# Softmax denominators of a transformer layer's masked attention: pair sums on VectorE and many ones-matmuls replaced by accumulating DMAs and one ones-matmul per run of eight steps

## Chip, cores, metric

One core of a Trainium2 chip. The metric is the device time of one execution of the whole kernel in microseconds (us), median of several runs.

## The reference, cut to what matters

Sixteen batches of 1024 nodes and 256 channels pass through three graph attention layers and one transformer layer with masked attention of eight heads. Only the latter's attention is changed.

```python
scores = jnp.einsum('fnhd,fmhd->fhnm', q, k) / jnp.sqrt(jnp.asarray(D, x.dtype))   # H = 8, D = 32
scores = jnp.where((adj > 0)[None, None, :, :], scores, -1e9)
attn = jax.nn.softmax(scores, axis=-1)
t = jnp.einsum('fhnm,fmhd->fnhd', attn, v).reshape(F, N, C)
```

The kernel computes exp(score) without a maximum, multiplies by the mask, and needs two sums over the 1024 keys: weights times values, and the weights alone (the denominator).

## The kernel before

A batch has four combinations of head group `g` (four heads) and half `hf` (512 queries), and each has eight steps `jt` of 128 keys. A step makes four 128x512 tiles of weights, two to a buffer `pa`. A *quad* is four matmuls (eight instructions in the trace), one for each head, side by side in the array's column groups.

```python
def paired(g, hf):
    return g == 1 or hf == 1          # three of the four combinations
...
for n in range(len(steps) + LAG):
    m = n - LAG                       # the value quad runs two steps behind the scores
    if m >= 0:
        both = not paired(g, hf)      # not paired: a ones quad at every step
        pe((1 + both) * 0.855, lambda: value(m, both), accs[g, hf], pas[m] + [va(jt)], ...)
        if not both and jt % 2:       # paired: a ones quad at every other step, from the pair sum
            pe(0.855, lambda: quad(accs[g, hf][1], jt, lambda r: ss[r // 2].t[:, r % 2, :], lambda r: ones, ...))
    ...                               # scores on TensorE, exp on ScalarE, mask on VectorE, into pas[n]
    if paired(g, hf) and jt % 2:
        sums[n] = [r_sums.new() for _ in range(2)]
        for ss, p0, p1 in zip(sums[n], pas[n - 1], pas[n]):
            dve(tt_us(2 * HALF), lambda: nc.vector.tensor_add(ss.t, p0.t, p1.t), [ss], [p0, p1])
```

(`...` marks cuts.) Nothing is emitted at once: `pe`, `dve`, `act`, `dma` record work with a planned duration, and a list scheduler at build time chooses each engine's fixed order from these and from constants (`BIAS` is its weight for changes of the array's mode; `GATS`, `VALUES`, `STEPS`, `FEED` spread each stage over the batches). Batches overlap: while one is in its attention, others are in graph attention or in the feed-forward part. The attentions of two batches hardly overlap, because keys, values and the transposed input have one buffer each.

## Time and profile before

| | before |
|---|---|
| time, median | 4240.8 us (4238.5 to 4245.0) |
| busy: TensorE, VectorE, ScalarE, GpSimd | 98%, 88%, 54%, 8% of the span |
| ones quads | 320, of 0.86 us each |
| pair additions on VectorE | 384, 457 us |
| DMA engines, mean of 16 | 22% |

The lines behind this table are in the prediction. It is read as one full engine, TensorE, with VectorE close behind and the DMA engines largely free: it invites moving additions to the DMA engines.

### The profile page before, as it was taken

The page shows a single profiled execution, that of the slowest core. Times are in us where ns is not written, and L with a number is a line of the kernel's source. Part 1 is how long each engine was busy: PE and PEld are TensorE (multiplying, and loading weights), DVE is VectorE, ACT ScalarE, POOL GpSimd, SP SyncE. Part 2 cuts the span into 40 slices and gives each one's busy share as a digit, 9 for nine tenths or more (in the row PEclk, how much of TensorE's full clock was granted, in tenths as well). Part 3 has the DMA queues.
Part 4 walks back from the last instruction along what each step waited for, and adds up shares of the span by engine and source line. Part 5 has one row for each costly group of instructions (what it writes and reads, how often), then busy time and mean ns, then how long its engine had stood idle before and what let it go on. Part 6 is the DMA issues. An engine that isn't in the chain of part 4 may idle for free.

```text
span 4234.8 us, 68471 instructions
## 1 busy us (share of the span) xinstructions
PE 4144.4 (98%) x24738; PEld 2385.9 (56%) x24738; DVE 3713.0 (88%) x6786; ACT 2307.1 (54%) x5041; POOL 351.7 (8%) x391
## 2 busy tenths in 40 slices
PE   7999999999999999999999999999999999999997
PEld 3746466564655646556464665646556465564642
DVE  7589898997989889898998989989898898988977
ACT  2445555554655645556555555656556455565564
POOL 0000010010100100001000100101001000010000
PEclk9999999999999999999999999999999999999998
DMA  3121222212222122221212222122212222212131
GB/s 103 50 66 36 76 66 66 56 46 70 68 75 53 50 66 61 81 63 56 60 48 75 66 66 56 50 66 71 76 52 60 56 60 81 64 52 60 47 82 39
DMA packets 180682, 263.82 MB, mean 62 GB/s; under 512 B 41328, under 2 KB 76400, under 8 KB 180336
## 3 DMA queue, kind: packets, MB, share of 16 engines
q1 hardware_dynamic: 180336, 259.36, 22.2%
q8 instruction: 198, 3.24, 0.3%
q14 instruction: 148, 1.21, 0.1%
HBM read 91.03 MB, written 33.95 MB: 30 GB/s over the span
## 4 chain that ended last, share of the span: by engine, by line
PE 73%; DVE 12%; ACT 7%; issue 3%; DMA 3%; POOL 2%; SPq 1%; DVEq 0%; ACTq 0%; POOLq 0%
PE bank L787 19%; PE bank L1094 12%; PE bank L861 9%; PE sc L1221 9%; PE bank L1327 5%; PE bank L871 5%; PE bank L663 4%; PE bank L460 4%; PE sc L1010 4%; DVE pa L1254 3%; DVE pt L760 2%; POOL rstd L412 2%; ACT hn L431 2%; ACT hna L431 2%; PE sc L1046 2%
## 5 line engine op out<-in xcount | busy, mean ns | idle before, releaser
L1245 ACT ACTIVATE pa<-sc 128x512 f32<-128x512 f32 x2048 | 1093.7, 608 | 610.3 <-PE sc L1221 524.7
L1254 DVE TENSOR_TENSOR pa<-pa,mask 128x1024 f32<-128x1024 f32 x1024 | 1220.2, 1215 | 48.5 <-ACT pa L1245 48.4
L760 DVE SCALAR_TENSOR_TENSOR pt<-row,e,mask 128x512 f32<-128x512 f32 x1536 | 1054.9, 744 | 90.7 <-DMA row<-rd 55.8
L787 PE MATMUL bank<-qb,pt 128*128 128x257 f32 x4096 | 940.9, 382 | 1.0 <-DVE pt L760 0.5
L787 PEld LDWEIGHTS bank<-qb,pt 128*128 128x128 f32 x4096 | 767.7, 190 | 197.5 <-ACT pa L1245 40.0
L1221 PE MATMUL sc<-qs,ks 128*128 128x512 f32 x2048 | 682.0, 446 | 2.9 <-ACT pa L1245 2.1
L1094 PE MATMUL bank<-pa,va 128*32 128x512 f32 x4096 | 533.0, 597 | 3.6 <-DVE pa L1254 3.2
L861 PE MATMUL bank<-pt,qb 128*32 128x512 f32 x4096 | 515.4, 595 | 7.3 <-DVE pt L760 6.7
L1221 PEld LDWEIGHTS sc<-qs,ks 128*128 128x128 f32 x2048 | 363.6, 188 | 237.1 <-ACT pa L1245 93.7
L1269 DVE TENSOR_TENSOR sums<-pa,pa 128x1024 f32<-128x1024 f32 x384 | 457.0, 1214 | 0.3 <-PE bank L1094 0.2
L663 PE MATMUL bank<-w_aug,hT 128*128 128x259 f32 (+1 forms) x1536 | 374.3, 388 | 4.3 <-ACT e L674 3.6
L815 ACT ACTIVATE ex<-bank,rec 128x256 f32<-128x256 f32 x256 | 122.1, 477 | 437.5 <-DVE rec L807 396.1
L663 PEld LDWEIGHTS bank<-w_aug,hT 128*128 128x128 f32 x1536 | 286.2, 191 | 74.0 <-issue 12.8
L412 POOL TENSOR_TENSOR rstd<-rstd,neg_half 128x4 f32<-128x4 f32 x160 | 203.1, 1272 | 1468.6 <-DVE rstd L409 1417.4
L861 PEld LDWEIGHTS bank<-pt,qb 128*32 128x32 f32 x4096 | 127.1, 109 | 310.0 <-issue 214.5
L871 PE MATMUL bank<-pt,e 128*32 128x512 f32 x2048 | 292.1, 592 | 0.0
L1094 PEld LDWEIGHTS bank<-pa,va 128*32 128x32 f32 x4096 | 116.2, 109 | 267.7 <-issue 208.7
L1010 PE MATMUL sc<-hTa,wqkv_sb 128*128 128x512 f32 x512 | 240.1, 596 | 4.6 <-ACT hTa L995 4.6
L431 ACT ACTIVATE hn<-xt,mv,rstd 128x256 f32<-128x256 f32 x384 | 206.3, 601 | 40.4 <-DVE mv L421 39.6
L892 ACT COPY ot<-bank 128x512 f32<-128x512 f32 x128 | 74.8, 586 | 257.7 <-PE bank L861 215.3
L1094 PE MATMUL bank<-sums,ones 128*32 128x512 f32 x1536 | 208.0, 596 | 0.8
L403 DVE BATCH_NORM_STATS2 stg<-xt 128x6 f32<-128x256 f32 x512 | 205.4, 414 | 3.2
(107 smaller groups left out, 3993.7 us busy)
## 6 DMA issues: line engine op xcount, KB each, us to landing
row<-rd SPq DMA_DIRECT2D x192, 256.0 KB
ks<-hi SPq DMA_DIRECT2D x512, 64.0 KB
ks<-lo SPq DMA_DIRECT2D x512, 64.0 KB
qs<-hi SPq DMA_DIRECT2D x512, 64.0 KB
qs<-lo SPq DMA_DIRECT2D x512, 64.0 KB
xt<-in_x_dram SPq DMA_DIRECT2D x32, 512.0 KB
x<-xt SPq DMA_DIRECT2D x32, 512.0 KB
xr<-x SPq DMA_DIRECT2D x64, 256.0 KB
```

The lines of the kernel that those rows point to most:

```text
L431: lambda: nc.scalar.activation(dst, src, func, bias=bias, scale=scale),
L663: nc.tensor.matmul(g.t[:, : C + 3 * H], hT.t[:, ct, k * P : (k + 1) * P], w_aug[l][:, ct, :], start=ct == 0, stop=ct == CT - 1,)
L760: lambda: nc.vector.scalar_tensor_tensor(pt.t, row.t, e3[:, 2, jt // TH, h, jt % TH : jt % TH + 1], mask[:, jt, hf * HALF : (hf + 1) * HAL ...
L787: nc.tensor.matmul(g.t[:, : D + 1], pts[jt].t[:, k * P : (k + 1) * P], qb[:, jt, 0, :], start=jt == 0, stop=jt == NT - 1,)
L861: nc.tensor.matmul(g.t[u * D + d : u * D + d + D3, :], qb[:, j, h + u, d : d + D3], pts[u][j - jt].t, start=j == 0, stop=j == NT - 1,)
L871: nc.tensor.matmul(gd.t[c : c + D3, :], one(jt + k, h + u).to_broadcast([P, D3]), pts[u][k].t, start=jt == 0, stop=jt == NT - 2,)
L1010: nc.tensor.matmul(sc.t, wqkv_sb[:, ct, c0 : c0 + P], hT.t[:, ct, hf * HALF : (hf + 1) * HALF], start=ct == 0, stop=ct == CT - 1,)
L1094: nc.tensor.matmul(ac.t[r * D3 : (r + 1) * D3, :], columns(r), of_head(r), start=first, stop=last,)
L1221: nc.tensor.matmul(scs[r - r0].t, ks.t[:, r, jt * P : (jt + 1) * P].bitcast(F32R), q.t[:, r, :].bitcast(F32R), start=True, stop=True,)
L1245: lambda: nc.scalar.activation(pt.t[:, v, :], sc.t, AF.Exp, scale=1.0 / math.sqrt(D3)),
L1254: lambda: nc.vector.tensor_mul(pt.t, pt.t, mask[:, jt : jt + 1, i0 : i0 + HALF].to_broadcast([P, 2, HALF]),),
L1269: lambda: nc.vector.tensor_add(ss.t, p0.t, p1.t),
```

## The change

Its intent: let the DMA engines add the eight steps' weights in SBUF, so that VectorE has no pair sums and TensorE multiplies by ones once per combination, 64 quads instead of 320.

```diff
-BIAS = 0.516
+BIAS = 0.211
-    GATS = (0.0, 0.388), (0.388, 0.271), (0.659, 0.201)
-    VALUES, STEPS, FEED = (1.132, 0.099), (1.231, 0.63), (2.355, 0.252)
+    GATS = (0.0, 0.375), (0.375, 0.244), (0.619, 0.227)
+    VALUES, STEPS, FEED = (0.94, 0.302), (1.242, 0.561), (2.172, 0.546)
...
+        RUN = 8
...
+                first = jt % RUN == 0
+                if first:
+                    sums[g, hf] = [r_sums.new() for _ in range(2)]
+                for ss, pt in zip(sums[g, hf], pas[m]):
+                    if first:
+                        dma(1.5, lambda: nc.sync.dma_start(ss.t, pt.t), [ss], [pt])
+                    else:
+                        dma(2.4, lambda: nc.gpsimd.dma_start(ss.t, pt.t, accum_op=ALU.add),
+                            [ss], [pt], us=1.1, engine="pool")
                 pe(
-                    (1 + both) * 0.855,
+                    0.855,                         # the value quad alone
...
-                if not both and jt % 2:
-                    ss = sums[m]
+                if jt % RUN == RUN - 1:
+                    ss = sums[g, hf]               # one ones quad per combination
...
-                if paired(g, hf) and jt % 2:       # the pair additions on VectorE
-                    ...
```

(Long calls are joined to one line and cuts are marked.)

More of the change, by code (lines that the diff above doesn't have):

```diff
@@ L1090, in attention, with quad @@
         pas, accs, sums = {}, {}, {}
-        def quad(ac, jt, of_head, columns, first, last):
+        def quad(ac, of_head, columns, first, last):
             for r in range(HG):
@@ L1100, in quad @@
                 )
-        def value(n, both):
-            g, hf, jt = steps[n]
-            for ac in accs[g, hf][: 1 + both]:
-                quad(
-                    ac,
-                    jt,
-                    lambda r: pas[n][r // 2].t[:, r % 2, :],
-                    lambda r: (
-                        ones
-                        if ac is accs[g, hf][1]
-                        else va.t[:, jt, (g * HG + r) * D3 : (g * HG + r + 1) * D3]
-                    ),
-                    jt == 0,
-                    jt == NT - 1,
-                )
-        def paired(g, hf):
-            return g == 1 or hf == 1
+        RUN = 8
         rec.stream(b + STEPS[0], STEPS[1])
@@ L1131, in attention @@
                     accs[g, hf] = [r_bank.new(), r_bank.new()]
-                both = not paired(g, hf)
-                pe(
-                    (1 + both) * 0.855,
-                    lambda: value(m, both),
-                    accs[g, hf],
+                first = jt % RUN == 0
[3 more added lines that the diff above has]
+                    if first:
+                        dma(
+                            1.5,
+                            lambda: nc.sync.dma_start(ss.t, pt.t),
+                            [ss],
+                            [pt],
+                        )
+                    else:
+                        dma(
+                            2.4,
+                            lambda: nc.gpsimd.dma_start(ss.t, pt.t, accum_op=ALU.add),
+                            [ss],
+                            [pt],
+                            us=1.1,
+                            engine="pool",
+                        )
+                pe(
+                    0.855,
+                    lambda: quad(
+                        accs[g, hf][0],
+                        lambda r: pas[m][r // 2].t[:, r % 2, :],
+                        lambda r: va.t[:, jt, (g * HG + r) * D3 : (g * HG + r + 1) * D3],
+                        jt == 0,
+                        jt == NT - 1,
+                    ),
+                    [accs[g, hf][0]],
                     pas[m] + [va(jt)],
@@ L1145, in attention @@
                             accs[g, hf][1],
-                            jt,
                             lambda r: ss[r // 2].t[:, r % 2, :],
                             lambda r: ones,
-                            jt == 1,
+                            jt == RUN - 1,
                             jt == NT - 1,
@@ L1263, in attention @@
                             )
-                if paired(g, hf) and jt % 2:
-                    sums[n] = [r_sums.new() for _ in range(2)]
-                    for ss, p0, p1 in zip(sums[n], pas[n - 1], pas[n]):
-                        dve(
-                            tt_us(2 * HALF),
-                            lambda: nc.vector.tensor_add(ss.t, p0.t, p1.t),
-                            [ss],
-                            [p0, p1],
-                        )
         watch(b_rec, b_rec.t, 1)
```

## The prediction

> **What bounds the kernel now.** I read the page first: shares of busy time, then the chain that ended last, then the costliest groups.
>
> ```profile
> PE 4144.4 (98%) x24738; PEld 2385.9 (56%) x24738; DVE 3713.0 (88%) x6786; ACT 2307.1 (54%) x5041; POOL 351.7 (8%) x391
> q1 hardware_dynamic: 180336, 259.36, 22.2%
> PE 73%; DVE 12%; ACT 7%; issue 3%; DMA 3%; POOL 2%; SPq 1%; DVEq 0%; ACTq 0%; POOLq 0%
> ```
>
> TensorE (PE) is busy for 98% of the span, and 73% of the chain is its own work. VectorE (DVE) follows at 88% and has its own part of the chain; GpSimd (POOL) and the DMA engines are mostly free. So time taken off TensorE should come off the end, as long as nothing else becomes the bound. Since busy time of matmuls overlaps, I take their real cost from the timeline, not from the groups. The groups (each shape apart) give the counts:
>
> ```profile
> L1269 DVE TENSOR_TENSOR sums<-pa,pa 128x1024 f32<-128x1024 f32 x384 | 457.0, 1214 | 0.3 <-PE bank L1094 0.2
> L1094 PE MATMUL bank<-sums,ones 128*32 128x512 f32 x1536 | 208.0, 596 | 0.8
> L1094 PE MATMUL bank<-pa,ones 128*32 128x512 f32 x1024 | 142.3, 592 | 0.0
> ```
>
> The matrices of ones form the softmax denominators: 1536 matmul instructions from pair sums that VectorE makes (three of the four head group and half combinations) and 1024 straight from the weights (the fourth). The timeline of TensorE in the middle of the run gives the pace:
>
> ```profile
> 2054.19 1.04 PE L1094 MATMUL bank<-pa,va 128*32 128x512 f32 x8
> 2055.05 1.04 PE L1094 MATMUL bank<-pa,ones 128*32 128x512 f32 x8
> 2055.91 1.04 PE L1094 MATMUL bank<-pa,va 128*32 128x512 f32 x8
> 2056.77 1.04 PE L1094 MATMUL bank<-pa,ones 128*32 128x512 f32 x8
> ```
>
> Columns are start, duration, engine, line, operation, tiles, shapes, count. The duration shown is 1.04 us, but the next group of eight (a quad: four heads, two instructions each) starts 0.86 us later. A quad costs **0.86 us** of TensorE.
>
> The last view is again TensorE's timeline, at a batch boundary, for the scores (the attention's first product):
>
> ```profile
> 2009.99 0.73 PE L1221 MATMUL sc<-qs,ks 128*128 128x512 f32 x2
> ...
> 2218.77 1.27 PE L1221 MATMUL sc<-qs,ks 128*128 128x512 f32 x4
> ...
> 2265.92 0.73 PE L1221 MATMUL sc<-qs,ks 128*128 128x512 f32 x2
> ```
>
> One batch's 32 attention steps take from 2010 to 2220, some 210 us; then 46 us pass before the next batch's first score. Other layers' work fills TensorE all the while. The mean is 4240/16 = 265 us a batch, or 210/32 = 6.6 us a step inside the attention. That matters for the rival below.
>
> **What the Trainium skill says.**
> 1. "DMA: Bandwidth & Descriptors", section "Rules for kernel authors": an accumulating DMA is issued from GpSimd, and reads its destination and writes it later, so that another accumulate into the same bytes must wait for the first one's semaphore. Each total is then a serial chain of eight transfers. The trace before has no accumulating DMA; no run shows it yet.
> 2. The same page, "Issuing engines are not separate DMA queues": transfers from GpSimd share the 16 engines with those from SyncE. The existing 22.2% must be added to the new load.
> 3. The same page, "Anatomy of one DMA — SWDGE (gpsimd) path": about 2.0 us fixed plus bytes over 436 GB/s. The trace agrees with the rate: in the start-up loads of the adjacency (512 KB each, as large as one accumulate) the DMA view of 20 to 36 us, in slices of 0.4 us, reads
>
> ```profile
> GB/s 243 300 294 225 230 225 246 415 384 451 440 389 440 379 461 266 102 20 0 0 0 0 0 0 0 21 72 297 389 410 190 128 113 138 154 251 369 364 394 358
> ```
>
> so 380 to 460 GB/s at best; I use 420.
> 4. "SBUF — State Buffer", "Who interferes with whom": a VectorE operation with two SBUF inputs contends with GpSimd's reads; descriptor generation needs the write side (the page calls it inferred). VectorE runs almost nothing but such operations here, so I expect little blocking of the new issues; no run shows it yet.
>
> **The change part by part.**
> *Removed from TensorE.* Before: (1536 + 1024)/8 = 320 quads of ones. After: one per head group and half, 4 x 16 batches = 64. Removed: 256 x 0.86 = **220 us**, all on the path that sets the end: 4240 - 220 = 4020.
> *Removed from VectorE.* 384 additions at 1.19 us busy each, 457 us: 3713 - 457 = 3256, 81% of 4020. In the stretches where the chain runs over VectorE this keeps TensorE fed, but TensorE's idle time is only 4235 - 4144 = 90 us, so it can be worth 90 us at most; I count 20.
> *Added to GpSimd.* Per batch 4 runs x 8 steps x 2 tiles = 64 transfers, 8 of them plain copies from SyncE and 56 accumulates: 896 accumulates in all. At the 1.1 us the program itself plans for an issue, 986 us; with 352 that is 1338 us, 33%. Not a bound.
> *Added to the DMA engines.* A copy moves 512 KB: 0.524 MB/420 GB/s = 1.25 us. An accumulate must read source and destination: I estimate twice that, 2.5 us (the program plans 2.4). Per batch 56 x 2.5 + 8 x 1.25 = 150 us. Existing: 22.2% of 265 = 59 us. Sum 209 us of a 251 us batch, 83%. Not over, but high, and an estimate.
> *Moved.* Planning constants are retuned, above all a smaller penalty (0.516 to 0.211) on mode changes of the array, which lets the schedule change modes more often. The program's table puts a change at about 0.1 us; I allow 20 us in all, an estimate without a view behind it.
>
> *The serial chain.* For each total: issue (1.1 us), 2.5 us of data, 1 to 2 us until the semaphore, thus about 5 us to the next. The two totals of a step overlap, but share engines: 2 x 2.5 = 5.0 us a step if nothing else moves, and 5.0/(1 - 0.22) = 6.4 us with SyncE's traffic at its mean share. A batch has 28 accumulating steps and 4 openings (wait for the closing quad, then a copy; I take 6 us): 28 x 6.4 + 24 = 203 us. With the 46 us between attentions this is 249 us, against TensorE's 4020/16 = 251. The two are **level** by my estimate, and that sets my range. The margin is 28 x 16 = 448 us of run time for each microsecond a step is longer, once the chain is the bound. Some overlap of the batch gap with the last run's tail helps; queueing hurts. Two engines level to 1% never mesh perfectly in a fixed instruction order: I add 80 us of waiting.
>
> Sum: 4240 - 220 - 20 + 20 + 80 = **4100 us**, 3.3% less.
>
> **The rivals.**
> *A: the accumulate is slower than planned and the chain becomes the bound.* For it: the order of instructions is fixed at build time from planned times; the weights' ring has six tiles, three steps, and a tile is now held until its transfer has landed, so that ScalarE and then TensorE stall behind a late one. The mean of all transfers in this trace is only 259 MB in 0.222 x 4235 us, 276 GB/s; at that rate an accumulate takes 3.8 us, a step 7.6 us plus SyncE's share, and a batch at least 28 x 7.6 + 24 + 46 = 283 us: 4530 us. Against it: those are mostly short packets; the new ones have 4 KB rows, and the 512 KB loads ran at 380 to 460.
> *B: the transfers delay others.* Row broadcasts from DRAM feed VectorE ("DMA row<-rd" already ends 55.8 us of VectorE's idle time, 31 times), and GpSimd, in order, now blocks on landings while rstd work queues behind it. For: 192 row loads and 160 rstd steps; 1 us each exposed would be 352 us. Against: TensorE always has work of another batch, and before the change it waited 12 us or less for anything. I would expect a quarter exposed: about 90 us, total 4110 to 4200 together with my waiting term.
> *C: nothing gets in the way.* TensorE stays at 98%: 4000 to 4030.
>
> **Range and chances.** C gives the lower end, 3990 with some of VectorE's relief. The centre, 4100, is level balance with some waiting. B alone lands near 4150 to 4200, about no change being 4155 to 4325. A starts at about 4350 and is open above. I weigh C 0.3, the centre 0.3, B 0.22, A 0.18. The constants in the diff (1.1, 2.4 and retuned spans) look like measured and fitted ones, which speaks against A; the close balance speaks for leaving it a fair share. That gives faster 0.70, same 0.14, slower 0.16, and 3990 to 4380 as a range for eight in ten.
>
> **What would show each step.** Right: 512 matmul instructions with ones instead of 2560, at 0.86 us a quad; no additions into sums on VectorE; VectorE busy about 3260; TensorE busy near 3920 and still 95% or more; DMA share near 80% of the attention's stretches; accumulates into one tile 5 to 6.5 us apart; scores of a batch within 210 us. Wrong by rival A: TensorE busy falls under 92%, ScalarE waits for DMA on pa, accumulates into one tile over 7 us apart, DMA near 90% throughout. Wrong by B: VectorE's wait for row grows from 56 us to several hundred, or its wait for rstd from 54 us. If accumulates cost clearly under 2.5 us of the engines, the result is C. The prediction fails if TensorE's work doesn't fall by the 220 us, or if GpSimd's issue costs 3 us instead of 1.1 (896 x 3 = 2700 us, and 6 us a step by itself).

## The result, and the profile after

4672.2 us (4667.0 to 4683.0, four runs) against 4240.8: ratio **1.1019**, 95% interval 1.0997 to 1.1042. The change is 10% slower; 3.3% faster had been predicted, and the time lies far outside the range. (A ratio here is the mean time of one kernel's runs over that of the other's of the same rounds, so not quite the ratio of the medians quoted.)

The page of the changed kernel: engines, DMA queues (packets, MB, share of 16 engines), the chain of waits by engine and by line, three groups, and the issues of the accumulates (count, KB each, us from issue to landing).

```profile
PE 4223.9 (90%) x22690; PEld 2371.7 (51%) x22690; DVE 3328.0 (71%) x6402; ACT 2331.7 (50%) x5041; POOL 1079.1 (23%) x1287
q0 software_dynamic: 129024, 469.82, 53.1%
q1 hardware_dynamic: 198768, 326.48, 23.4%
DMA 32%; PE 32%; DVE 20%; issue 7%; SPq 4%; ACT 3%; POOL 2%; DVEq 0%; ACTq 0%; POOLq 0%
L1250 ACT ACTIVATE pa<-sc 128x512 f32<-128x512 f32 x2048 | 1110.4, 602 | 861.3 <-DMA sums<-pa 489.5
L1127 POOL DMA_DIRECT2D sums<-pa x896 | 780.6, 877 | 2706.8 <-DVE pa L1259 894.1
L1094 PE MATMUL bank<-sums,ones 128*32 128x512 f32 x512 | 130.6, 693 | 76.1 <-DMA sums<-pa 55.3
sums<-pa POOLq DMA_DIRECT2D x896, 512.0 KB, 5.8
```

The work went where it was meant to: 512 ones instructions instead of 2560, VectorE 385 us less busy. But TensorE's share fell from 98% to 90%, and its own part of the chain from 73% to 32%; the DMA engines have 32% of the chain, by line mostly `sums<-pa`. ScalarE now stands idle 489.5 us for accumulates that have not released a `pa` buffer. The queue of the accumulates gives their price: 53.1% of 4673.4 us over 896 is **2.77 us of all 16 engines** each.

TensorE's busy time itself did not fall. It rose by 80 us, though 2048 matmul instructions are gone; in e1_drop (below), with the same instructions, it is 3945 us. The clock granted to TensorE was lower: 0.956 of full speed in the mean, against 0.995 before and 0.993 in e1_drop, and a ones matmul on `sums` took 693 ns in the mean, 596 before. If all of TensorE's work lay on the path, this would cost at most 3945 x (0.993/0.956 - 1) = 153 us, an estimate. The clock is lower in the slower runs of this series (0.978 in e14_three_quarters); no run parts it from the waits, so its share of the loss stays open.

The clearest view is the end of the run. Only the last batch's attention is left there, and nothing competes with it. GpSimd's timeline (start, duration of the issue, ..., idle before and what ended it), then the DMA view of 4565 to 4585 us:

```profile
4564.67 0.86 POOL L1127 DMA_DIRECT2D sums<-pa  x1 [1.59 <-DVE pa L1259]
4567.23 0.86 POOL L1127 DMA_DIRECT2D sums<-pa  x1 [1.69 <-DVE pa L1259]
4569.98 0.86 POOL L1127 DMA_DIRECT2D sums<-pa  x1 [1.89 <-DVE pa L1259]
4572.72 0.86 POOL L1127 DMA_DIRECT2D sums<-pa  x1 [1.88 <-DMA sums<-pa]
4575.48 0.86 POOL L1127 DMA_DIRECT2D sums<-pa  x1 [1.90 <-DMA sums<-pa]
```

```profile
DMA packets 1042, 3.83 MB, mean 191 GB/s; under 512 B 112, under 2 KB 112, under 8 KB 1040
q0 software_dynamic: 1040, 3.80, 99.0%
sums<-pa POOLq DMA_DIRECT2D x8, 512.0 KB, 5.0
```

One accumulate starts about every 2.75 us, the engines are 99% busy with them alone, and 512 KB per 2.75 us are the 191 GB/s. A step needs two, so no step of an attention can be shorter than 5.5 us, whatever TensorE does. The same stretch, from the last batch's first exp to the end, in the view by windows (length; busy us and instructions of each engine; TensorE's granted clock; DMA share; GB/s), before and after:

```profile
4060.00:4235.00 175.00, 149.12 (x688) 57.74 (x688) 141.86 (x217) 88.36 (x166) 13.04 (x11) 0.94 0.22 58
```

```profile
4418.00:4673.00 255.00, 171.30 (x558) 59.43 (x558) 116.12 (x178) 89.45 (x165) 58.33 (x66) 0.80 0.80 172
```

It takes 80 us longer with fewer instructions for TensorE and VectorE (TensorE's busy time grows, at a granted clock of 0.80 against 0.94); the DMA engines go from 22% to 80%. That is 80 of the 439 us between the two spans. The other 357 us are in the fifteen batches before: from the first exp of batch 0 to that of batch 15, ScalarE's timeline gives 3839 us before (255.9 a batch) and 4195 us after (279.7).

What the other transfers suffer shows in the list of waits (engine, line, what it waited for: us, times, longest), before:

```profile
DVE pt L760 <- DMA row<-rd: 55.8, 31, 8.1
DVE mv L421 <- POOL rstd L412: 54.2, 53, 1.1
DVE xr L1385 <- DMA xr<-x: 17.6, 17, 3.6
```

and after:

```profile
DVE xr L1381 <- DMA xr<-x: 226.5, 35, 10.5
DVE mv L421 <- POOL rstd L412: 126.0, 91, 3.8
DVE pt L760 <- DMA row<-rd: 116.6, 38, 8.0
PE sc L1226 <- DVE lo L1022: 108.3, 17, 9.2
```

### The profile page after: what moved, and what is told of

Its sections match the earlier page's. It is cut to its first block, busy times and chain, and to the rows that moved or that the text cites. A ratio compares the mean times of both kernels' runs of the same rounds, so it can differ in the third digit from the quotient of the medians.

```text
span 4673.4 us, 67023 instructions
## 1 busy us (share of the span) xinstructions
PE 4223.9 (90%) x22690; PEld 2371.7 (51%) x22690; DVE 3328.0 (71%) x6402; ACT 2331.7 (50%) x5041; POOL 1079.1 (23%) x1287
## 3 DMA queue, kind: packets, MB, share of 16 engines
q0 software_dynamic: 129024, 469.82, 53.1%
## 4 chain that ended last, share of the span: by engine, by line
DMA 32%; PE 32%; DVE 20%; issue 7%; SPq 4%; ACT 3%; POOL 2%; DVEq 0%; ACTq 0%; POOLq 0%
DMA sums<-pa 23%; DVE pt L760 9%; PE bank L787 6%; DVE pa L1259 5%; PE bank L1094 4%; SPq L1031 4%; PE bank L861 4%; DMA out_dram<-xr 4%; PE bank L663 3%; PE sc L1010 3%; PE sc L1226 3%; PE bank L460 3%; DMA row<-rd 2%; PE bank L1323 2%; DMA xr<-x 2%
## 5 line engine op out<-in xcount | busy, mean ns | idle before, releaser
L1250 ACT ACTIVATE pa<-sc 128x512 f32<-128x512 f32 x2048 | 1110.4, 602 | 861.3 <-DMA sums<-pa 489.5
L1127 POOL DMA_DIRECT2D sums<-pa x896 | 780.6, 877 | 2706.8 <-DVE pa L1259 894.1
L760 DVE SCALAR_TENSOR_TENSOR pt<-row,e,mask 128x512 f32<-128x512 f32 x1536 | 1055.5, 740 | 190.4 <-DMA row<-rd 116.6
L787 PE MATMUL bank<-qb,pt 128*128 128x257 f32 x4096 | 958.4, 384 | 3.8 <-DVE pt L760 3.8
L1226 PE MATMUL sc<-qs,ks 128*128 128x512 f32 x2048 | 737.0, 459 | 184.2 <-DVE lo L1022 108.3
L1094 PE MATMUL bank<-pa,va 128*32 128x512 f32 x4096 | 620.9, 616 | 43.1 <-DVE pa L1259 39.8
L663 PE MATMUL bank<-w_aug,hT 128*128 128x259 f32 (+1 forms) x1536 | 423.7, 424 | 62.6 <-ACT e L674 27.3
L663 PEld LDWEIGHTS bank<-w_aug,hT 128*128 128x128 f32 x1536 | 309.8, 210 | 190.0 <-ACT qb L685 57.0
L1010 PE MATMUL sc<-hTa,wqkv_sb 128*128 128x512 f32 x512 | 263.3, 639 | 3.7 <-ACT pa L1250 2.3
L1381 DVE TENSOR_TENSOR xr<-xr,row_c 128x512 f32<-128x512 f32 x64 | 43.5, 680 | 226.5 <-DMA xr<-x 226.5
L1094 PE MATMUL bank<-sums,ones 128*32 128x512 f32 x512 | 130.6, 693 | 76.1 <-DMA sums<-pa 55.3
```

The source lines that it names most:

```text
L663: nc.tensor.matmul(g.t[:, : C + 3 * H], hT.t[:, ct, k * P : (k + 1) * P], w_aug[l][:, ct, :], start=ct == 0, stop=ct == CT - 1,)
L760: lambda: nc.vector.scalar_tensor_tensor(pt.t, row.t, e3[:, 2, jt // TH, h, jt % TH : jt % TH + 1], mask[:, jt, hf * HALF : (hf + 1) * HAL ...
L787: nc.tensor.matmul(g.t[:, : D + 1], pts[jt].t[:, k * P : (k + 1) * P], qb[:, jt, 0, :], start=jt == 0, stop=jt == NT - 1,)
L1010: nc.tensor.matmul(sc.t, wqkv_sb[:, ct, c0 : c0 + P], hT.t[:, ct, hf * HALF : (hf + 1) * HALF], start=ct == 0, stop=ct == CT - 1,)
L1094: nc.tensor.matmul(ac.t[r * D3 : (r + 1) * D3, :], columns(r), of_head(r), start=first, stop=last,)
L1127: lambda: nc.gpsimd.dma_start(ss.t, pt.t, accum_op=ALU.add),
```

## The experiments

Theory **S**: the accumulates occupy the 16 DMA engines, and during an attention these become the bound. Rivals: **L**, the serial latency of issue, landing and semaphore in each chain; **C**, the retuned constants; **P**, a fixed order planned from too low costs. In runs that leave out or falsify the sums, the result is wrong, and two details are changed alike: the reciprocal of the denominator becomes an addition of 1 (no division by zero), and the switch to the general fallback is off. Each ratio is to the kernel before.

### The accumulates left out, or made plain copies

```diff
 e1_drop:   the else branch with nc.gpsimd.dma_start(..., accum_op=ALU.add) is removed
 e2_plain:
-    nc.gpsimd.dma_start(ss.t, pt.t, accum_op=ALU.add)
+    nc.gpsimd.dma_start(ss.t, pt.t)
```

> The 896 accumulates are left out, everything else of the change stays (order, constants, the 128 copies, one closing quad per run); the result is wrong on purpose. Theory S (the accumulates themselves, as transfers, cost the time): TensorE becomes the bound again, 4020 to 4090 us. Theory C (the retuned constants or the new order of TensorE are bad in themselves): above 4250 us.

Measured: 4068.9 us, 0.9596. The rest of the change keeps what was expected of it: 172 us less, of the 220 worked out. C is out as a cause of the loss.

> The same 896 transfers, from GpSimd and in the same serial chain, but as plain copies without addition; wrong result on purpose. Theory S, in the form that the read-modify-write occupies the 16 DMA engines twice as long as a copy (2.75 us against about 1.3): queue share falls from 53% to about 27%, time 4050 to 4250 us. Rival L (the serial latency of issue, landing and semaphore, not the occupation, sets the pace): landing falls only by 1 to 1.5 us, time stays above 4400 us.

Measured: 4155.6 us, 0.9800. The same 896 transfers in the same chains cost 87 us more than none; as accumulates they cost 603 us more. The page of this run:

```profile
q0 software_dynamic: 129024, 469.82, 29.4%
sums<-pa POOLq DMA_DIRECT2D x896, 512.0 KB, 3.5
```

29.4% of 4149.8 us over 896 is 1.36 us; an accumulate's 2.77 us is **2.03 times** a copy's. But landing fell too, from 5.8 to 3.5 us, and an issue from 0.86 to 0.53 us, so this run alone does not part S from L.

### The chains kept, the occupation varied

```diff
 e9_tiny, e13_half, e14_three_quarters with c = 8, 256, 384:
-    nc.gpsimd.dma_start(ss.t, pt.t, accum_op=ALU.add)
+    nc.gpsimd.dma_start(ss.t[:, :, :c], pt.t[:, :, :c], accum_op=ALU.add)
```

> The same 896 accumulates in the same serial chains and with the same waits, but each over 8 columns of 512 per half (about 1/64 of the bytes); wrong result on purpose. It keeps issue, landing and semaphore of every link and takes the engines' occupation away. Theory S (occupation of the 16 engines): within 2% of the run without accumulates, 4060 to 4150 us, although each link still takes some 3 us to land. Theory L (serial latency): above 4300 us.

Measured: 4083.9 us, 0.9632. Queue and landing (min, median, max) of this run:

```profile
q0 software_dynamic: 243712, 7.40, 9.8%
DMA to landing us min/median/max: 2.4/2.6/5.7
```

Every link still takes 2.6 us to land, with all its waits, plus 1.2 us of issue (0.86 in the change). With the occupation at 0.45 us, the chains cost 15 us in all over e1_drop. L is out in the sense that these fixed parts of a link are harmless by themselves.

> The change with accumulates over 256 of the 512 columns of each half; wrong result on purpose. Occupation should be about 1.4 us, as much as a whole plain copy's 1.36 us. If occupation alone decides, the time is that of the plain copies, 4130 to 4190 us; if reading and writing the destination costs more than the engines' time, above 4300 us.

> The same over 384 columns: occupation about 2.1 us. By the serial sum, a step is 2 x 2.1 us, over 0.77 with SyncE's share 5.5 us; 28 steps, 4 openings of 6 us and 67 us of gap are 245 us a batch, just under TensorE's 251: 4150 to 4350 us if there is a knee where the attention's transfers overtake TensorE's work; about 4400 us (halfway between 4156 and 4672) if the time grows in proportion to the occupation.

Measured: half the columns 4136.3 us (0.9751), three quarters 4363.2 us (1.0291). The occupations, from these queues, were higher than expected, 1.73 and 2.37 us; first half, then three quarters:

```profile
q0 software_dynamic: 243712, 234.94, 37.5%
```

```profile
q0 software_dynamic: 243712, 352.38, 48.8%
```

All runs with the order of the change, in order of occupation. The period is the mean distance between the first exps of successive batches (twelve in the middle), from ScalarE's timeline:

| run | occupation per transfer (queue share x span / 896) | landing, median | period of a batch | time |
|---|---|---|---|---|
| e1_drop | none | none | 246.9 us | 4068.9 us |
| e9_tiny | 0.45 us | 2.6 us | 245.1 | 4083.9 |
| e2_plain (copies) | 1.36 | 3.5 | 248.7 | 4155.6 |
| e13_half | 1.73 | 4.2 | 246.9 | 4136.3 |
| e14_three_quarters | 2.37 | 5.1 | 261.2 | 4363.2 |
| the change | 2.77 | 5.8 | 281.0 | 4672.2 |

There is a **knee** between 1.73 and 2.37 us. Below it the period stays at TensorE's 245 to 249 us; above it, 0.40 us more of occupation cost 309 us. If every one of the 896 waited its turn in full, it would be 358 us. Growth in proportion, the other expectation, would have put three quarters above 4400; the 4363 measured are nearer to the knee's range of 4150 to 4350, but 13 us outside it. The half run is 19 us faster than the copies though its transfers occupy the engines longer: occupation under the knee does not order these two, and what does stays open. Below the knee most of what the transfers cost lies in the last batch's attention, from its first exp to the end: 147 us in e1_drop, 185 in e9_tiny, 209 in e2_plain, 212 in e13_half. Landing grows along with occupation, so above the knee the two are not separate causes.

One batch in the middle of the run shows the two limits, in the view by windows: its attention (first exp to last), then the gap to the next batch's first exp. First e9_tiny, then the change:

```profile
1947.10:2135.40 188.30, 187.16 (x1095) 108.24 (x1097) 167.86 (x294) 111.39 (x244) 77.31 (x67) 1.00 0.38 79
2135.40:2192.10 56.70, 56.70 (x325) 35.63 (x318) 37.42 (x103) 31.90 (x73) 10.99 (x14) 1.00 0.42 103
```

```profile
2192.00:2414.60 222.60, 203.90 (x1123) 114.96 (x1123) 171.83 (x297) 112.62 (x243) 57.23 (x66) 0.96 0.84 184
2414.60:2477.40 62.80, 58.46 (x297) 33.83 (x292) 34.16 (x99) 32.49 (x73) 12.06 (x15) 0.92 0.59 134
```

In e9_tiny TensorE is busy throughout. In the change the attention is 34 us longer and the gap 6 us. Over twelve batches in the middle the DMA engines are busy for 85% of the attentions and 58% of the gaps, so they are not as full as at the end of the run (99%): that the attention waits for them rests on the runs above, which vary what they carry. The depth of the buffers is a rival that no run tested: six for `pa`, two for `sums`, one for keys and values in every run. Deeper ones might hide more of the engines' time.

### Constants and plan

```diff
 e3_consts: BIAS, GATS, VALUES, STEPS, FEED of the kernel before
 e4_plan:
-    2.4, ... us=1.1, engine="pool"
+    2.8, ... us=0.9, engine="pool"
-    queue[e] = max(at + 0.2, queue[e]) + x.moved          # a queue per issuing engine
+    queue["dma"] = max(at + 0.2, queue["dma"]) + x.moved  # one for all, and pass_on alike
```

> The change with the planning constants of the kernel before (mode penalty 0.516 and the old spans). Theory S: 4600 to 4750 us, as with the new ones. Theory C: below 4450 us, because the new constants were the harm.

> The change, its order planned with the measured costs: 2.8 us per accumulate instead of 2.4, 0.9 us per issue instead of 1.1, and one DMA queue shared by the issuing engines in the plan. Theory P (the fixed order was planned too optimistically and the stalls are its fault): below 4450 us. Theory S: 4550 to 4720 us, a gain of 2% at most, as the attention of a batch can't be faster than its transfers.

Measured: 4716.1 us (1.1111) and 4714.6 us (1.1115). The old constants are no better, and a plan that knows the real costs is a little worse. C is out, and P as far as three orders can show it: none of those by this planner hid the engines' time.

### The opening copies removed

```diff
 at step 0 of a run:
-    nc.sync.dma_start(ss.t, pt.t)                    # copy of the masked weights
+    nc.vector.tensor_mul(ss.t, pt.t, mask_of_step)   # the mask product written into the total
     (and the value quad of step 0 reads ss)
```

> The change without its 128 opening copies: VectorE writes the masked weights of step 0 straight into the total, and accumulates follow. Between two runs of accumulates some 12 us pass now, 3.2 us of it the landing of the copy. Theory S with serial openings: 4 x 3 us x 16 batches = 190 us less at most, 4480 to 4620 us. If the DMA engines' occupation alone sets the pace (56 x 2.77 us of accumulates a batch either way), only the 8 copies' 1.3 us count, 170 us at most and likely under 80: 4590 to 4670 us.

Measured: 4690.4 us (1.1049), no gain, a miss for both expectations. The new dependence shows in the list of waits:

```profile
POOL sums L1133 <- PE bank L1094: 575.6, 29, 39.3
```

The first accumulate into a total must now wait for the value quad that reads it. That took the place of the wait for the copy, so the run does not tell what shorter openings alone would bring.

### Fewer combinations by accumulates

```diff
-    return g == 1 or hf == 1                 # paired
+    return (g, hf) in ((0, 0),)              # e6_one; also (1, 0) in e7_two; also (0, 1) in e8_three
     these accumulate by DMA as in the change; the others keep VectorE's pair sums;
     constants of before, plan costs of e4_plan
```

> Only the first of the four head group and half combinations of a batch uses accumulating DMAs (the one that took eight quads of ones before); the others keep VectorE's pair sums; constants of before. Theory S: 14 accumulates a batch are 39 us of the engines in a 260 us batch, no bound; TensorE loses 7 quads x 16 x 0.86 us = 96 us: 4140 to 4190 us, faster than before. If any use of accumulates disturbs (waits of GpSimd's queue, order), 4240 us or more.

> Two of four combinations by accumulating DMAs (first half of each head group), two by pair sums; constants of before. TensorE loses 10 quads a batch, 138 us; serial time of an attention by the measured 44 us a run and 12 us an opening: 2 x 56 + 2 x 30 + 67 us of gap = 239 us, still under TensorE's 256. Theory S: 4100 to 4170 us.

> Three of four combinations by accumulating DMAs. TensorE loses 13 quads a batch, 179 us, and would allow 4060; the serial time of an attention is 3 x 56 + 30 + 67 = 265 us a batch, above that. Theory S: the turn comes here, 4150 to 4350 us, slower than with two. If throughput of the engines alone counted (42 x 2.77 + 67 = 183 us of 254), 4060 to 4120 us.

Measured: one 4247.3 us (1.0011), two 4358.8 (1.0275), three 4554.8 (1.0726); all four, with the same constants but the plan costs of the change, is e3_consts, 4716.1. The order of the three is as S has it, but each is above what I expected. The serial sum for two, 239 us a batch, was wrong: the period was 261.5 us. The two combinations with accumulates took 55.6 and 54.2 us from first exp to first exp, as counted (44 + 12), but the paired ones took 66.9 us, where 30 had been counted, and 84.8 with the gap, where 97 had. In a fixed order shared with two other batches a combination does not run at its own shortest time. What bounds these mixed kernels (the engines are busy 52% of the time in e7_two) stays open.

For one combination the engines were no bound on average (14.6% and 23.0% of their time). Its 224 accumulates were therefore left out, and its constants searched anew with the planner; the search was given to the kernel before as well, as a control:

```diff
 e10_one_drop:     e6_one without the accumulates (wrong on purpose)
 e11_one_tuned:    e6_one with BIAS = 0.687, STEPS = (1.199, 0.669), ... from a search
 e12_before_tuned: the kernel before with BIAS = 0.56, GATS = (0.0, 0.388), (0.388, 0.281), (0.659, 0.173),
                   VALUES, STEPS, FEED = (1.132, 0.042), (1.231, 0.63), (2.292, 0.18)
```

> The version with one combination by accumulates (4247 us, where 4140 to 4190 had been expected), without its 224 accumulates; wrong result on purpose. If the accumulates ate the 96 us that TensorE saves: 4140 to 4170 us. If VectorE (88% busy, its 384 pair additions stay) and the fixed order are what holds it: 4220 to 4250 us, as with them.

> One combination by accumulates, with planning constants searched anew for this load (mode penalty 0.687, other spans). If only the order kept the saved TensorE time from showing: 4150 to 4200 us, faster than before by 1 to 2%. If the accumulates themselves did: 4230 us or more.

> Control to the run above: the kernel before, its constants searched anew for as long. The search alone should bring at most 1%: 4195 to 4240 us. What the run with one combination gains beyond this is the accumulates' own.

Measured: 4228.0 us (0.9968), 4216.7 us (0.9940), 4190.2 us (**0.9880**). Chain and engines of e10_one_drop, then of e12_before_tuned:

```profile
PE 4142.9 (98%) x23842; PEld 2356.4 (56%) x23842; DVE 3716.7 (88%) x6786; ACT 2330.8 (55%) x5041; POOL 381.0 (9%) x391
PE 51%; DVE 32%; issue 5%; ACT 5%; DMA 3%; POOL 2%; SPq 1%; DVEq 0%; ACTq 0%
```

```profile
PE 4125.9 (99%) x24738; PEld 2394.1 (57%) x24738; DVE 3710.4 (89%) x6786; ACT 2325.9 (56%) x5041; POOL 311.4 (7%) x391
PE 89%; DVE 7%; issue 1%; DMA 1%; ACT 1%; SPq 0%; POOL 0%; DVEq 0%; ACTq 0%
```

Of the 96 us that one combination takes off TensorE, 13 show even with no accumulate at all. VectorE's part of the chain rises from 12% (before) to 32%: with its pair additions still there, and in this order, VectorE takes the bound over. The accumulates themselves cost the 19 us between e6_one and e10_one_drop. A better order helps the version with accumulates (4216.7) less than the kernel without (4190.2), whose chain is now 89% TensorE. **The fastest correct kernel of this study is the old one with new constants**, 1.2% ahead of before; one search of equal length each does not prove that the other could not be ordered better.

## Why the prediction was wrong, point by point

The mechanism that came true is my rival A, with 0.18 as its share; the centre held the same mechanism at a break-even that is not there. Two of its marks are met: TensorE busy under 92% (90), ScalarE waiting for DMA on `pa` (489.5 us). Two are nearly so: the engines are busy for 85% of the attentions, not near 90% throughout, and accumulates into one total are 2 x 3.40 = 6.8 us apart, short of the 7 I had set. That A's 283 us a batch lie so close to the measured 281 is luck: A took 3.8 us for an accumulate, where 2.77 were measured, and openings and a gap that were too short.

- **What TensorE and VectorE save**: right as work. 64 ones quads remain. e1_drop shows 172 us of the 220 counted on the path; VectorE's 3328 us are near the 3256 predicted. TensorE's busy time, predicted near 3920 us, is 3945 in e1_drop but 4224 in the change, at its lower clock.
- **GpSimd's issue**: 1.1 us was assumed, 0.86 us measured. Not a bound, right.
- **The accumulate's occupation**: estimated 2.5 us, "twice a copy". Twice is right (2.03), but the copy was too cheap: 1.25 us from the load rate, 1.36 measured. 2.77 instead of 2.5 is 11% more on the resource that turned out to bind.
- **The serial sum of a batch** is the step that failed, by its size: 249 us against TensorE's 251. GpSimd's timeline of the change gives its terms (batches 1 to 13, from issue to issue; an extra is a distance less the 3.4 us of an ordinary one):

| term | predicted | measured |
|---|---|---|
| 28 accumulating steps (56 transfers) | 28 x 6.4 = 179 us | 56 x 3.40 = 190 us |
| extra at openings within a batch | 3 x 6 = 18 | 3 x (12.3 - 3.4) = 27 |
| extra between batches | 6 + 46 = 52 | 67.1 - 3.4 = 64 |
| sum | 249 | 281 |

  All three are short. Openings and gap are so long in this order even without the engines' occupation: e9_tiny has 13.8 us at an opening and 63.3 between batches, where the change has 12.3 and 67.1. What the occupation stretched is the ordinary distance, 2.70 us there and 3.40 here: 36 us over the 52 of a batch, as much as the whole growth from 245 to 281. The gap (46 us from last score to first) was copied from the kernel before as if it were fixed; in the new order it is 57 us in e9_tiny and 67 in the change. Nor does a short gap alone help: e3_consts has 43 us, but its attention takes 242 us from first score to last, where the change's takes 213. The gap also contains the next batch's transfers of keys and queries, and these slow down: `qs<-lo` lands after 4.1 us here and after 2.0 us in e1_drop, and TensorE idles 108 us for `lo` ahead of the scores, some 7 us a batch, where the kernel before shows 0.7 in all.
- **The reading of the balance** failed with it. I wrote that each microsecond a step is longer costs 448 us once the chain is the bound, and then added 80 us of waiting for "level". With no slack, errors of 6, 50 and 23% in the three terms, all to the short side, went straight into the time: 281 - 249 = 32 us a batch is 480 us over fifteen batches, most of the whole error of 572. e14_three_quarters shows how sharp the knee is: 14% less occupation than in the change is 309 us.
- **The drain at the end** was left out: the last batch's attention has nothing to hide behind and takes 80 us longer.
- **Rival B** (transfers delay others): present but small in the waits it named. `row` went from 55.8 to 116.6 us, rstd from 54.2 to 126.0. The largest is one it did not name, the read-back `xr`, from 17.6 to 226.5 us.
- **"The constants look measured"** was a poor argument against A. The planned 2.4 us were under the real 2.77, and the planner kept a DMA queue per issuing engine, so that it could not see SyncE and GpSimd on the same 16 engines. With both mended (e4_plan) the kernel was no faster.

## What to carry to other kernels

Work moved to the DMA engines is not free just because their mean share is low: count, for the stage in which it falls, transfers times engine time (here an accumulating DMA took 2.03 times that of a copy) and compare it with what that stage may last, its serial gaps included. When such a sum comes out level with the present bound, expect the loss, not the gain, because nothing is left to absorb an estimate that is 13% short, as this one was. And when an engine is relieved in a kernel with a planned order, replan the old kernel for as long before crediting the change.

## What the Trainium skill lacked or had wrong

- "DMA: Bandwidth & Descriptors" says that accumulates go through GpSimd and must wait for one another, and names the add unit, but gives no duration for one that a kernel issues. Here 512 KB in float32 in SBUF, 128 partitions, occupied the 16 engines for 2.77 us against 1.36 us as a plain copy from the same queue, 191 GB/s when nothing else ran.
- Same page, "Anatomy of one DMA — SWDGE (gpsimd) path": about 2.0 us plus bytes over 436 GB/s gives an estimate of 3.2 us for 512 KB. The plain copies landed after a median of 3.5 us, near it; accumulates after 5.0 us with nothing else in flight but each other, 5.8 over the run. The smallest (8 columns in each half) landed after 2.6 us.
- Same section: descriptor generation is called small and variable. An accumulate's issue kept GpSimd 0.86 us with one row per partition and 1.19 to 1.20 us with two, a plain copy's 0.53 us with one.
- "SBUF — State Buffer", "Who interferes with whom", infers that VectorE's two-input operations do not hold up descriptor generation. The change's trace is in line with it: with VectorE 71% busy, the issues' median of 0.859 us is also their minimum.
